# Attention and mixture of experts on one core: regrouping TensorE's work for a pair of heads by array split

## The chip, the core and the metric

The kernel runs on one core of a Trainium2 chip. The metric is the device time of one execution in microseconds (us). Three runs of the kernel before the change are known, and one further execution was taken by the hardware profiler. The core's engines are TensorE (PE, with weight loads shown as PEld), VectorE (DVE), ScalarE (ACT), GpSimd (POOL), and SyncE (SP), which issues most DMAs. All data are 32-bit floats.

## The reference

The input has 4 batches of 1024 tokens of width 256. A layer is causal attention with 16 heads, a residual and a layer norm, then 16 experts of which each token uses 3, a residual and a layer norm. Cut to the attention, which is all that the change touches:

```python
proj = x @ W_in.T + b_in                      # q, k, v: 16 heads of 64
q, k = rope(q), rope(k)                       # y_lo = lo*cos + hi*sin, y_hi = hi*cos - lo*sin
att = softmax(mask(q @ k.T / 8))              # 1024 x 1024, lower triangle
y = att @ v
x = layernorm(x + (y @ W_out.T + b_out))
x = layernorm(x + experts(x))                 # top 3 of 16, 256 -> 512 -> 256
```

## The kernel before

Heads are worked in pairs (`hh` is 0 or 1), 8 pairs a batch, 32 pairs `n` in all. After them come the experts. The loop over `n` stands in `attention`; the order of TensorE and VectorE inside it is written out by hand (`tc.manual_schedule` for PE and DVE), ScalarE, GpSimd and SP follow their dependencies and the program's order. Names that are used below:

- `project(n, i, g)` (L282 matmul `pp`, L287 on VectorE, L293 on ScalarE) makes q (`i` = 0) or k (`i` = 1) of pair `n` for 512 tokens `g`: two 128*128 matmuls, a product with `sin` and, on ScalarE, a plain copy `raw`. DMAs swap the copy's 32-row quarters into `swq` or `swk`. `rotate` (L321, L326, GpSimd) multiplies the swapped copy by `cos` and adds.
- `scores(n, qcs)` works the row blocks `qc` (128 queries each) of a chunk: 64*128 matmuls into PSUM banks `s` (L385), at most 512 columns each, for both heads; then on VectorE a reduction per bank (L393) that masks, copies to `p` and finds the row's extreme; then the exponential with row sums on ScalarE (L408). `divide` takes the reciprocal on VectorE (L422) and scales on GpSimd (L425).
- `turn` (L444) transposes 32x32 blocks of `p` on VectorE into `t_last` (keys 512 and up) and `t_first` (keys below 512).
- `product(n, j)` (L465) multiplies by v for key block `j` in 32*64 parts of the array, and adds up over `j` = 7 to 0 in four banks `y_ps`, of which 256 of 512 columns are used. `close` copies them out (`yT`, L479).
- `values` (L335 `vv`, L340) makes v for a pair two ahead, which goes through memory `v_d` and comes back as `vr` (`spread`). `out` (L489 `oo`) multiplies by W_out, a quarter of the tokens at a time, and VectorE adds the result to `acc` (L571).
- `fill` puts operations of the router and the layer norm of the batch before (`todo`) in between; `scatter` issues the router's indirect DMAs on GpSimd.

`pp`, `s`, `vv` and `oo` share four PSUM banks (`ps_s`), handed out in turn; `y_ps` has the other four. A pair's chunks are (7), (6), (5), (4), (3, 2), (1, 0), one per step `k` of the loop:

```python
for k in range(n_slots):
    ...
    if here:
        ends = scores(n, chunks[k])
    ...
    if k in (3, 4) and here:
        product(n, 10 - k)
    ...
    if k == 5 and here:
        product(n, 5)
    ...
    if k < 2 and before:
        product(n - 1, 4 - 2 * k)
        product(n - 1, 3 - 2 * k)
```

So products 7, 6 and 5 of pair `n` stand between its own later chunks, and 4 to 0 between the first chunks of pair `n + 1` (0 in step 2).

Of the kernel before, what the change touches and what calls it, by code (L numbers as in the profile page):

```python
# [119 lines left out]
def attention(  # L120
    tc, ap_, ident, eps_t, zero, router, sums, v_d,
# [4 lines left out]
    with ExitStack() as ctx:  # L126
# [7 lines left out]
        vp = pool("a_v", 3)  # L134
# [4 lines left out]
        pp = pool("a_p", 6)  # L139
        tp = pool("a_t", 1)  # L140
        yp = pool("a_y", 2)
# [11 lines left out]
        def load_x(b, g):  # L153
            xts[b, g] = xp.tile([P, DC, 512], FP, tag="xT", name="xT")
            return nc.sync.dma_start(out=xts[b, g], in_=xT_v[b, :, :, ts(g, 512)])
# [12 lines left out]
        def load_v(n):  # L168
            wv[n] = wp.tile([P, DC, 2 * P], FP, tag="wv", name="wv")
            return nc.sync.dma_start(out=wv[n], in_=w_v[n % NP // 2])  # L170
# [18 lines left out]
        mask = cp.tile([P, 512], FP, tag="mask")  # L189
        nc.gpsimd.memset(mask[:, : 512 - P], 0.0)  # L190
        make_causal_mask(nc, mask[:, 512 - P :], BIG / SCALE)
# [71 lines left out]
        raws, swps = {}, {}  # L263

        def project(n, i, g, kind=None):


            b, p = divmod(n, NP)
            if i == 0:
                half = rot[n, 0, g] = qkp.tile([P, 512], FP, tag=f"rotq{g}", name="rotq")  # L270
                part = raw = qkp.tile([P, 512], FP, tag="rawq", name="rawq")
                whole = True
            else:
                whole = n == 0 or (n, 1) in rot
                if (n, 1) not in rot:
                    rot[n, 1] = qkp.tile([P, T], FP, tag="rotk", name="rotk")
                    raws[n] = qkp.tile([P, T], FP, tag="rawk", name="rawk", bufs=1)
                half, raw = rot[n, 1][:, ts(g, 512)], raws[n]
                part = raw[:, ts(g, 512)]
# [14 lines left out]
            if whole:  # L294

                if i == 0:
                    swp = swps[n, 0, g] = qkp.tile([P, 512], FP, tag="swq", name="swq")
                else:
                    if (n, 1) not in swps:
                        swps[n, 1] = qkp.tile([P, T], FP, tag="swk", name="swk", bufs=1)  # L300
                    swp = swps[n, 1]
                if i and n == 0:
                    swp, raw = swp[:, ts(g, 512)], part
                for r in range(4):
                    (nc.scalar if i and n == 0 and g else nc.sync).dma_start(
                        out=swp[ts(r, 32), :], in_=raw[ts(r ^ 1, 32), :]
                    )
# [56 lines left out]
        def scores(n, qcs, kind=None):  # L364
# [3 lines left out]
            for hh in range(2):  # L368
                pr = pp.tile([P, T], FP, tag="p", name="p")
                at = 0  # L370
                for qc in qcs:
                    probs[n, qc, hh] = pr[:, ds(at, (qc + 1) * P)]
                    at += (qc + 1) * P
            for qc in qcs:
                w = (qc + 1) * P
                for k0 in reversed(range(0, w, 512)):
                    n_k = min(512, w - k0)
                    for hh in range(2):

                        if qcs == (1, 0) and qc == 0:  # L380
                            s = parts[hh][4][:, 2 * P :]
                        else:
                            s = ps_s.tile([P, 512], FP, tag="s", name="s")
                        parts.append((qc, hh, k0, n_k, s))
                        nc.tensor.matmul(  # L385
                            s[:, :n_k], lhsT=rot[n, 0, qc // 4][ts(hh, KD), ts(qc % 4, P)],
                            rhs=k[ts(hh, KD), ds(k0, n_k)], start=True, stop=True,
                        )
            nmax, ends = {}, []
            for qc, hh, k0, n_k, s in parts:  # L390
# [4 lines left out]
                    in1=mask[:, 512 - n_k :] if diag else zero[:, :n_k], scale=SCALE,  # L395
# [4 lines left out]
                if kind:  # L400
                    after(i, kind)
                order["scores"] = i
                if last:
                    pr = probs[n, qc, hh]
                    if hh == 0:
                        rsum = sp.tile([P, 2], FP, tag="rsum", name="rsum")
                        ends.append((qc, rsum))
                    order["exp"] = nc.scalar.activation(  # L408
                        pr, pr, AF.Exp, bias=m, scale=-1.0, accum_out=rsum[:, hh : hh + 1]
                    )  # L410
            return ends

# [73 lines left out]
        def out(n, h):  # L486
            ps = ps_s.tile([P, 2, D], FP, tag="s", name="oo")
            for v in range(2):
                nc.tensor.matmul(  # L489
                    ps[:, v, :], lhsT=st[n][:, ts(2 * h + v, P)], rhs=wo[n],  # L490
                    start=True, stop=True,
                )
            return accs[n // NP][:, ds(2 * h, 2), :D], ps
# [6 lines left out]
        chunks = [(7,), (6,), (5,), (4,), (3, 2), (1, 0)]  # L500
        n_slots = len(chunks)
        n_pairs = B * NP
        for i, g in ((0, 1), (1, 0), (1, 1), (0, 0)):
# [11 lines left out]
        with tc.manual_schedule(engines={mybir.EngineType.PE, mybir.EngineType.DVE}):  # L515
            for n in range(n_pairs + 2):
                b, p = divmod(n, NP)
                if n == 2:
                    load_router(Later(nc.vector, DVE, todo))
                for k in range(n_slots):  # L520
                    here, before, ahead = (one_of(n + i) for i in (0, -1, 1))
                    part, ends, last = None, [], "scores"
                    if before:
                        scatter(1 if k == 0 else 2 if k == 2 and here else 0)
                        if k == 0:
                            fill(ACT, 4.0)
                    if k == 2 and n <= n_pairs:
                        fill(DVE, 2.2, port=0.9)
                        fill(ACT, 4.0)
                    if k == 1:  # L530
                        fill(DVE, 0.7, True)
                    if here:
                        ends = scores(n, chunks[k])

                    m, kk = divmod(n * n_slots + k - 2, n_slots)
                    rows = [(qc, h) for h in (1, 0) for qc in chunks[kk] if qc >= 4 * h]

                    def turns(last):
                        qc, h = rows.pop(0)
                        for hh in range(2 if one_of(m) else 0):  # L540
                            turn(m, qc, hh, h, last)
                            last = "turn"
                        return last

                    if k == 2:
                        last = turns(last)

                    if k == 5:
                        fill(DVE, 0.6, True)
                    if k in (2, 5) and ahead:  # L550
                        project(n + 1, 0, int(k == 2), last)
                        last = "part"
                    if k == 2 and before:
                        product(n - 1, 0)
                        close(n - 1)
                    if k in (3, 4) and here:
                        product(n, 10 - k)
                    if k in (0, 3, 4, 5) and one_of(n - 1 - (k == 0)):
                        part = out(n - 1 - (k == 0), (k - 3) % 4 if k else 3)
                    if k in (3, 5):  # L560
                        fill(PE, 0.5 if k == 3 else 2.7)
                    if k == 5 and here:
# [776 lines left out]
```

## Time and profile before

| | |
|---|---|
| median of 3 runs | 1595.21 us (1595.2 to 1602.86) |
| profiled execution | 1580.36 us, its span 1578.5 us |
| granted TensorE clock in it | 0.982 |
| first pair's start to last pair's products | about 20 to 1126 us |
| experts, final norm and store | to 1578.5 us |

The views are read as follows. The page's first part gives busy time of each engine and its share of the span. The chain follows the work that ended last back from the end, so its shares name who set the time. A table by stage gives busy time in cut-out stretches. The timeline gives start and length of merged groups; the matmuls' ends are modelled, and one that starts before the last one's end overlaps it in the array's pipeline. An array split is written before the shape: 128*128, 64*128 or 32*64.

### The profile page before, as it was taken

What the parts mean: (1) busy time and instruction counts of PE and PEld (TensorE: products, weight loads), DVE (VectorE), ACT (ScalarE), POOL (GpSimd) and SP (SyncE); (2) the same over time, 40 slices, a digit from 0 to 9 for tenths busy, and PEclk for the clock granted to TensorE, in tenths of its full rate; (3) what the DMA queues carried; (4) which work ended last, traced back from release to release, by engine and by line L of the source; (5) the groups of instructions that cost most, each with busy time, mean ns of one, the idle gap of its engine ahead of it and who ended that gap; (6) DMA issues with size and microseconds to landing.
All of it is one profiled execution on the core that took longest, in us unless ns stands there. A gap on an engine that the chain in (4) does not pass through costs nothing.

```text
span 1578.5 us, 52463 instructions
## 1 busy us (share of the span) xinstructions
PE 1502.1 (95%) x20832; PEld 1047.0 (66%) x20832; DVE 1171.5 (74%) x3675; ACT 730.8 (46%) x1694; POOL 979.2 (62%) x928
## 2 busy tenths in 40 slices
PE   7999999999999999999999999999898999999970
PEld 4566666666666666666665666665687888888860
DVE  4888888898899999878999999889756333333324
ACT  3555555556555555655555557554431222222214
POOL 3775665775565677767766766678277843434435
PEclk9999999999999999999999999999999999999985
DMA  6464445546444554564465445545598998989866
GB/s 197 136 161 130 129 128 144 151 129 186 117 121 129 146 145 132 147 193 132 134 174 141 132 132 155 165 120 144 180 315 268 364 273 227 262 246 272 244 187 220
DMA packets 120041, 280.34 MB, mean 178 GB/s; under 512 B 21344, under 2 KB 64608, under 8 KB 108256
## 3 DMA queue, kind: packets, MB, share of 16 engines
q1 hardware_dynamic: 99872, 250.05, 52.9%
q0 software_dynamic: 19584, 26.62, 8.0%
q8 instruction: 166, 2.72, 0.8%
q14 instruction: 83, 0.68, 0.1%
q10 hardware_dynamic: 336, 0.27, 0.1%
HBM read 186.81 MB, written 61.09 MB: 157 GB/s over the span
## 4 chain that ended last, share of the span: by engine, by line
PE 86%; DVE 6%; issue 3%; DMA 3%; POOL 1%; ACT 1%; SPq 0%; ACTq 0%; POOLq 0%; DVEq 0%
PE y_ps L465 18%; PE s L385 17%; PE pp L282 14%; PE ps L1089 10%; PE ps L1073 10%; PE oo L489 7%; PE vv L335 7%; PE ps L1037 1%; DVE t_first L444 1%; DVE p L393 1%; PE lg_ps L706 1%; DMA sums<-y,ids 1%; DVE o_stats L1209 1%; POOL xs L803 1%; DMA vr<-v_d 1%
## 5 line engine op out<-in xcount | busy, mean ns | idle before, releaser
L425 POOL TENSOR_SCALAR p<-p,rinv 128x512 f32<-128x512 f32 (+7 forms) x512 | 374.6, 746 | 336.7 <-DVE rinv L422 291.9
L408 ACT ACTIVATE p<-p,nmax 128x512 f32<-128x512 f32 (+7 forms) x512 | 391.7, 766 | 411.9 <-DVE nmax L393 410.0
L385 PE MATMUL s<-rotk,rotq 64*128 64x512 f32 (+3 forms) x1536 | 309.6, 514 | 2.6 <-DVE rotk L318 2.0
L393 DVE CUSTOM_DVE_ANT_0 p<-s,mask 128x512 f32<-128x512 f32 (+3 forms) x512 | 224.2, 485 | 82.2 <-PE s L385 82.0
L444 DVE STREAM_TRANSPOSE t_first<-p 128x512 f32<-128x512 f32 (+3 forms) x512 | 276.1, 583 | 8.9 <-PE y_ps L465 8.8
L1104 POOL DMA_INDIRECT sums<-y,ids x104 | 163.5, 1572 | 181.1 <-DVE y L1100 121.3
L282 PE MATMUL pp<-xT,wqk 128*128 128x512 f32 x512 | 251.4, 614 | 9.2 <-DMA wqk<-in_w_qk_dram 5.5
L1078 ACT ACTIVATE hid<-ps,w 128x256 f32<-128x256 f32 (+1 forms) x224 | 89.7, 456 | 296.8 <-issue 244.3
L465 PE MATMUL y_ps<-t_first,vr 32*64 32x160 f32 (+2 forms) x8192 | 209.9, 338 | 4.3 <-DVE t_first L444 2.2
L465 PEld LDWEIGHTS y_ps<-t_first,vr 32*64 32x64 f32 x8192 | 165.9, 130 | 58.5 <-issue 44.2
L385 PEld LDWEIGHTS s<-rotk,rotq 64*128 64x128 f32 x1536 | 139.2, 186 | 97.7 <-issue 53.7
L1073 PE MATMUL ps<-xg,w 128*128 128x256 f32 (+1 forms) x896 | 191.7, 367 | 6.8 <-DVE xg L1040 6.8
L1094 DVE TENSOR_TENSOR y<-ps,w 128x512 f32<-128x512 f32 (+1 forms) x56 | 36.6, 653 | 212.9 <-PE ps L1089 175.4
L1089 PE MATMUL ps<-w,hid 128*128 128x256 f32 x832 | 188.8, 379 | 0.5 <-ACT hid L1078 0.5
L393 DVE CUSTOM_DVE_ANT_0 p<-s,zero,nmax 128x512 f32<-128x512 f32 x256 | 181.9, 748 | 2.9 <-PE s L385 0.7
L1073 PEld LDWEIGHTS ps<-xg,w 128*128 128x128 f32 x896 | 158.7, 192 | 25.5 <-DVE xg L1040 7.6
L282 PEld LDWEIGHTS pp<-xT,wqk 128*128 128x128 f32 x512 | 90.0, 190 | 126.1 <-issue 63.0
L1089 PEld LDWEIGHTS ps<-w,hid 128*128 128x128 f32 x832 | 157.2, 190 | 21.6 <-ACT hid L1078 0.7
L465 PEld LDWEIGHTS y_ps<-t_last,vr 32*64 32x64 f32 x7424 | 105.1, 130 | 76.5 <-issue 50.0
L489 PE MATMUL oo<-wo,yT 128*128 128x256 f32 x512 | 141.0, 398 | 2.6 <-ACT yT L479 1.4
L465 PE MATMUL y_ps<-t_last,vr 32*64 32x96 f32 (+3 forms) x7424 | 126.9, 248 | 0.5 <-DVE t_last L444 0.4
L803 POOL DMA_INDIRECT xs<-acc,slots x96 | 97.2, 1012 | 43.9 <-issue 21.8
(187 smaller groups left out, 1726.9 us busy)
## 6 DMA issues: line engine op xcount, KB each, us to landing
w<-in_wall_dram SPq DMA_DIRECT2D x56, 1154.0 KB
vr<-v_d SPq DMA_DIRECT2D x256, 128.0 KB
vr<-v_d SPq DMA_DIRECT2D x128, 256.0 KB
swq<-rawq SPq DMA_DIRECT2D x256, 64.0 KB
v_d<-v SPq DMA_DIRECT2D x128, 128.0 KB
swk<-rawk SPq DMA_DIRECT2D x124, 128.0 KB
x<-xs SPq DMA_DIRECT2D x48, 264.0 KB
wqk<-in_w_qk_dram SPq DMA_DIRECT2D x32, 256.0 KB
```

What stands on the lines that cost most here:

```text
L282: nc.tensor.matmul(ps, lhsT=wqk[n][:, c, i, :], rhs=xts[b, g][:, c, :], start=(c == 0), stop=(c == DC - 1),)
L385: nc.tensor.matmul(s[:, :n_k], lhsT=rot[n, 0, qc // 4][ts(hh, KD), ts(qc % 4, P)], rhs=k[ts(hh, KD), ds(k0, n_k)], start=True, stop=True,)
L393: i = nc.vector.tensor_tensor_reduce(out=probs[n, qc, hh][:, ds(k0, n_k)], in0=s[:, :n_k], in1=mask[:, 512 - n_k :] if diag else zero[:, : ...
L408: order["exp"] = nc.scalar.activation(pr, pr, AF.Exp, bias=m, scale=-1.0, accum_out=rsum[:, hh : hh + 1])
L425: order["divide"] = router.behind = nc.gpsimd.tensor_scalar(pr, pr, rinv[:, hh : hh + 1], 1.0, ALU.mult, ALU.mult)
L444: order["turn"] = router.on_dve = after(nc.vector.transpose(turned[n][h][:, hh, :, ds(i - 4 * h, n_j, step=7 - 4 * h), :], probs[n, i, hh] ...
L465: nc.tensor.matmul(st[n][a][ts(hh, KD), ds(32 * j, 32 * (TC - j))], lhsT=v[ts(a, 32), c * 8 + 2 * u + jh % 2, ts(hh, KD)], rhs=t[ts(a, 32) ...
L489: nc.tensor.matmul(ps[:, v, :], lhsT=st[n][:, ts(2 * h + v, P)], rhs=wo[n], start=True, stop=True,)
L803: i = nc.gpsimd.indirect_dma_start(out=self.xs, out_offset=bass.IndirectOffsetOnAxis(ap=st["slots"][:, r, c : c + 1], axis=0), in_=acc[:, ...
L1073: nc.tensor.matmul(ps[:, f - f0, :], lhsT=w[:, ds(c * FF + f * P, P)], rhs=xg[:, c, :n], start=(c == 0), stop=(c == DC - 1),)
L1089: nc.tensor.matmul(ps[:, h, :], lhsT=hid[:, f, ts(h, P)], rhs=w[:, ds(W2_AT + f * D, D)], start=(f == 0), stop=(f == FC - 1),)
L1104: s = behind(nc.gpsimd.indirect_dma_start(out=sums_of(t), out_offset=bass.IndirectOffsetOnAxis(ap=ids[:, h : h + 1], axis=0), in_=y[:, h, ...
```

## The change

The six steps of a pair become four groups. The five chunks 4, 3, 1, 0 and 2 are multiplied in one run, with product 7 ahead of it; the 128*128 work of that part follows in one run, then products 6, 5 and 4; products 3 to 0 stand in the next pair, after chunk 6. `multiply` (the matmuls) is split from `scores` (reductions and exponentials), and `bank` puts the scores of row blocks 1 and 0 and the 128 diagonal columns of block 4 into unused columns of the `y_ps` banks. Exponentials can be held back (`hold`, `release`) so that they are issued later on ScalarE. `out` takes two pairs at once and adds both up in PSUM, so that VectorE adds to `acc` once for two pairs; `plan` says where. The divisions of chunk (1, 0) are issued in the next pair. Each swapped half of k goes out by itself. To fit memory, buffers change: the probabilities have one buffer for each chunk and head, `wv`, one half of `xT`, one half of the rotated q and the swapped q are single, `yT` has three, mask and zeros share a tile, and three tiles of the router share one (`wide`).

```diff
-        pp = pool("a_p", 6)
+        pp = pool("a_p", 1)
...
-        yp = pool("a_y", 2)
+        yp = pool("a_y", 3)
...
+            part = qkp.tile([P, 512], FP, tag="raw", name="raw")
...
+                swp = swps[n, 0, g] = qkp.tile([P, 512], FP, tag="swq", name="swq", bufs=1)
...
+            for r in range(4):
+                (nc.scalar if i and n == 0 and g else nc.sync).dma_start(
+                    out=swp[ts(r, 32), :], in_=part[ts(r ^ 1, 32), :]
+                )
...
+        def bank(n, qc, hh, k0):
+            y = st.get(n)
+            if qc == 4 and k0:
+                return y[2 + hh][:, 3 * P :], False
+            if qc == 1:
+                return y[hh][:, 2 * P :], False
+            if qc == 0:
+                return y[2 + hh][:, 2 * P : 3 * P], False
+            return ps_s.tile([P, 512], FP, tag="s", name="s"), True
...
-        def out(n, h):
+        def out(pairs, h):
             ps = ps_s.tile([P, 2, D], FP, tag="s", name="oo")
             for v in range(2):
...
+                for n in pairs:
+                    nc.tensor.matmul(
+                        ps[:, v, :], lhsT=st[n][:, ts(2 * h + v, P)], rhs=wo[n],
+                        start=(n == pairs[0]), stop=(n == pairs[-1]),
+                    )
...
+                if here:
+                    ends = scores(n, (7,), multiply(n, (7,)), hold)
+                    release(1)
+                if before:
+                    divide(n - 1, ends10, last)
+                if ahead and n > 0:
+                    project(n + 1, 1, 0, last)
...
+                last = turns(n - 1, [(3, 0)], last)
+                for o in outs.get((n, 0), []):
+                    parts.append(out(*o))
...
+                if here:
+                    ends = scores(n, (6,), multiply(n, (6,)))
+                last = turns(n - 1, [(2, 0), (1, 0), (0, 0)], last)
...
+                if ahead:
+                    project(n + 1, 1, 1, last)
...
+                for j in reversed(range(4 if before else 0)):
+                    product(n - 1, j)
+                if before:
+                    close(n - 1)
...
+                last = turns(n, [(7, 1)], last)
+                if n <= n_pairs:
+                    fill(DVE, 2.4, port=0.6)
...
+                if here:
+                    ends5 = scores(n, (5,), multiply(n, (5,)), hold)
+                    release(1)
+                last = turns(n, [(7, 0)], last)
+                if ahead:
+                    project(n + 1, 0, 1, last)
+                release()
+                if here:
+                    product(n, 7)
...
+                if here:
+                    ends4 = scores(n, (4,), multiply(n, (4,)))
+                    p3 = multiply(n, (3,))
+                    small = multiply(n, (1, 0))
+                    ends32 = scores(n, (3, 2), p3 + multiply(n, (2,)), hold)
+                    divide(n, ends5, "scores")
+                    ends10 = scores(n, (1, 0), small, hold)
+                    release(2)
+                if vals:
+                    values(m, vals[0])
+                release(2)
+                last = turns(n, [(6, 1)], last)
+                if here:
+                    divide(n, ends4, last)
+                if ahead:
+                    rotate(n + 1, 0, 1)
+                last = turns(n, [(5, 1)], last)
+                if ahead:
+                    project(n + 1, 0, 0, last)
...
+                product_out()
...
+                last = turns(n, [(4, 1)], last)
+                if here:
+                    divide(n, ends32, last)
...
+                last = turns(n, [(6, 0)], last)
+                if vals:
+                    values(m, vals[1])
...
+                last = turns(n, [(5, 0), (4, 0)], last)
+                if ahead:
+                    rotate(n + 1, 0, 0)
...
+                if here:
+                    for j in (6, 5, 4):
+                        product(n, j)
+                if p < 2:
+                    fill(DVE, 2.0 - 0.6 * p)
```

## The prediction

> **What bounds the kernel now.** I read the page first: engine shares and the chain.
>
> ```profile
> PE 1502.1 (95%) x20832; PEld 1047.0 (66%) x20832; DVE 1171.5 (74%) x3675; ACT 730.8 (46%) x1694; POOL 979.2 (62%) x928
> PE 86%; DVE 6%; issue 3%; DMA 3%; POOL 1%; ACT 1%; SPq 0%; ACTq 0%; POOLq 0%; DVEq 0%
> ```
>
> TensorE carries 86% of the chain. The whole-span share mixes attention and experts, so next comes the table by stage, cut at the first product of four neighbouring pairs.
>
> ```profile
> core 0: us, PE busy (x) PEld busy (x) DVE busy (x) ACT busy (x) POOL busy (x), PEclk, DMA share, GB/s
> 105.20:139.00 33.80, 33.80 (x588) 21.18 (x586) 29.19 (x89) 18.24 (x44) 21.36 (x22) 1.00 0.44 121
> sum 135.00, PE 135.00 PEld 84.64 DVE 116.60 ACT 72.78 POOL 85.45; mean PE 33.75 PEld 21.16 DVE 29.15 ACT 18.19 POOL 21.36
> ```
>
> A pair takes 33.75 us and TensorE is busy for all of it; VectorE has 4.6 us to spare, GpSimd 12.4. TensorE's waits between 100 and 1060 us say the same:
>
> ```profile
> PE pp L282 <- DVE nmax L393: 2.2, 4, 1.4
> PE y_ps L465 <- issue: 0.2, 1, 0.2
> ```
>
> So a pair is as long as TensorE's instruction stream, and anything off TensorE is worth nothing until it makes TensorE wait. What can the stream lose without losing matmuls? The timeline of TensorE (start, length, line):
>
> ```profile
> 283.59 1.98 PE L282 MATMUL pp<-xT,wqk 128*128 128x512 f32 x4
> 285.41 1.03 PE L489 MATMUL oo<-wo,yT 128*128 128x256 f32 x4
> 286.37 1.05 PE L465 MATMUL y_ps<-t_last,vr 32*64 32x96 f32 x64
> ...
> 292.09 1.19 PE L465 MATMUL y_ps<-t_last,vr 32*64 32x128 f32 x63
> 293.02 0.29 PE L465 MATMUL y_ps<-t_first,vr 32*64 32x160 f32 x1
> ...
> 293.04 1.35 PE L465 MATMUL y_ps<-t_first,vr 32*64 32x160 f32 x63
> 294.32 1.77 PE L385 MATMUL s<-rotk,rotq 64*128 64x384 f32 x8
> 296.03 1.98 PE L282 MATMUL pp<-xT,wqk 128*128 128x512 f32 x4
> 297.94 3.07 PE L465 MATMUL y_ps<-t_first,vr 32*64 32x192 f32 x128
> 300.94 1.56 PE L385 MATMUL s<-rotk,rotq 64*128 64x256 f32 x8
> ```
>
> Add start and length and compare with the next start. pp ends at 285.57 and oo, of the same split (128*128), starts at 285.41, 0.16 before. oo ends at 286.44 and the product, of another split (32*64), starts at 286.37, only 0.07 before. A change of split costs 0.09 us there. Inside products it costs more: product 4 ends at 293.28 and product 3 starts at 293.02, 0.26 before; product 3 ends at 294.39 and the scores start at 294.32, 0.07 before: 0.19 us.
>
> **The gain.** I write S7 for the score chunk of row block 7, Y7 for product 7, pp/vv/oo for the 128*128 work. Before, a pair's ring is S5, pp, Y0, S4, Y7, oo vv, S3 S2, Y6, oo vv, S1 S0, pp oo, Y5, S7, oo pp, Y4 Y3, S6, pp, Y2 Y1: 18 changes. After: S5, pp, Y7, S4 S3 S1 S0 S2, vv pp oo vv, Y6 Y5 Y4, S7, pp oo, S6, pp, Y3 to Y0: 11 (the change's words say 12). In the built programs' order on TensorE I count 572 changes before and 352 after, 220 fewer, 7 for each of 31 pairs. Of the 7, four are ends of scores or 128*128 work (4 x 0.09 = 0.36) and three ends of product runs (3 x 0.09 to 0.19 = 0.27 to 0.57). Together 0.63 to 0.93, taken at 0.80 (the product seams are nearer to the measured 0.19), so 31 x 0.80 = 25 us, between 20 and 29. Matmuls are as many as before: two pairs added up in PSUM still need all of theirs.
>
> **What could take it back: the burst.** Four score banks feed all scores and 128*128 work. Five chunks in a run, with no product between them, must find their banks emptied by VectorE. The change gives them help: S1, S0 and the diagonal 128 columns of S4 go to free columns of the product banks. I walk one pair from the start of S5 (t = 0). TensorE, start to start from the timeline and the chain of waits: S5 1.49, pp 1.91, Y7 0.66, S4 1.39, S3 plus S2 1.70, S1 plus S0 0.85, vv, pp and oo 1.73 to 1.82 each. VectorE, from its own timeline at the same place before:
>
> ```profile
> 301.67 0.42 DVE L393 CUSTOM_DVE_ANT_0 p<-s,mask 128x256 f32<-128x256 f32 x1 [2.21 <-PE s L385]
> ...
> 303.88 1.30 DVE L444 STREAM_TRANSPOSE t_last<-p 128x512 f32<-128x512 f32 x2
> 305.10 0.71 DVE L287 SCALAR_TENSOR_TENSOR rotq<-pp,bqk,sin 128x512 f32<-128x512 f32 x1
> ```
>
> VectorE begins S5 0.73 after TensorE (300.94 to 301.67, after idling 2.21), leaves it at 2.94 and needs 1.22 for a transpose pair. Hence:
>
> ```
> t (us)      TensorE                 VectorE
> 0 - 4.06    S5, pp, Y7              S5 0.73-2.94, transposes -4.16, rotq -4.87
> 4.06- 8.00  S4 S3 S1 S0 S2          S4 4.87-6.8, S3 -8.0
> 8.00-15.1   vv pp oo vv             S2 8.2-9.1, S1 S0 -10.3, transposes 6,5 (last half) -11.9, rotq -12.6, 4 -13.2
> 15.1-17.7   Y6 Y5 Y4                sum -14.2, six 128x512 transposes (0.65 each) -18.1
> 17.7-       S7                      S7 from 18.75 (1.05 after its start)
> ```
>
> Where TensorE needs a bank: the second half of S3 takes pp's, free when ScalarE's copy of it ends (4.87 + 0.05 + 0.69 = 5.6), and TensorE is there at 5.45 + 0.43 = 5.9. S2 takes S4's two, free at 6.1 and 6.8, needed at 7.26. The first vv takes S3's, free at 7.4, needed at 8.0. Y4 needs the transpose that ends at 13.2, at about 16.8. S7's reductions find VectorE free 0.65 early. In the second half of the pair the tightest is S6's last bank, freed by the output sum 0.3 ahead. So: no wait, but margins of 0.3, 0.5, 0.6 and 0.3 us on a TensorE that has had none to lose.
>
> **Other parts.** Output sums: 128 become 68, 60 x 0.659 = 40 us off VectorE; off the path, worth 0, but without them the last margin (0.65) is gone. The reciprocal of S5's sums now stands behind the reductions of S4, S3 and S2 on VectorE, so GpSimd starts that division at 9.2. Behind it stand 640's division and the rotation of the next q: 9.2 + 2 x 0.90 + 2 x 0.80 + 2 x 1.275 = 15.2 against S7 at 17.7. The other q rotation, after the divisions and up to three scatters of 1.01, ends by 23.5 and is needed at S3 of the next pair, near 38. The divisions of S1 and S0 wait for the next S7 and end by 25.5, for transposes near 28. Swapped k goes out in eight DMAs of 64 KB, not four of 128; at some 0.6 us an issue in the trace, 2.4 us more on SP, which issues some 30 a pair. The swap buffer for q is single now, so four DMAs on SP wait for GpSimd's rotation (15.2); behind them are v stores, the next pair's swapped k and v loads, of which the first to be needed, v for Y7, has over 10 us. All of these at 0; if a cover fails each costs what its margin lacks, 0 to 1 us a pair. Fill work of 2.0 and 1.4 us is put right before S7 in two pairs of three batches, where the margin is 0.65: 0 to 1.2 us each, 0 to 7 us, taken at 3. First pair and last: the first product rows come later, past the wait for v that holds TensorE 2 us at 55 us; the last pair has less 128*128 work over the same VectorE chain (TensorE was already idle some 6 us there): 0, between -4 and +4. The experts after it start earlier by the same amount.
>
> **A rule against it.** The Trainium skill, TensorEngine Tiling (Array Packing), PSUM Bottleneck, says that tiling makes TensorE faster but not the evacuation of PSUM, which may then be the bottleneck. Taken at its word the run is paced by its reductions (1.8 + 2.2 + 1.1 us in the table's rows against 3.94 of TensorE, 1.1 a pair), and the sum would be 31 x (1.1 - 0.8) = +9, 1604 us. The walk gives 0 for it, because 7 us of vv, pp and oo follow at once, in which VectorE catches up.
>
> **Sum.** The profiled execution took 1580.4 (span 1578.5); 1580.4 - 25 + 3 = 1558. The median of the three runs, 1595.2, is 14.8 above it, and the trace does not show why; I carry the difference over: 1595.2 - 22 = 1573. Its own range: -29 - 4 to -20 + 7 + 4, so 1562 to 1586.
>
> **Rivals.**
> 1. The margins are partly eaten: one of the 0.3 us margins misses by 0.5 to 0.8 us in each pair, and the saving goes into a wait for VectorE. Then 1588 to 1603. For: four margins below 0.7. Against: VectorE's rows repeat to a few hundredths from pair to pair. Chance 0.12.
> 2. Slower: the run starves for banks. Place: S3's second half to the first vv. In the first pair, where no products lie between the chunks, 8 matmuls of S7 run 329 ns apart, not 200: about 0.8 us more for a chunk. If S4, S3 and S2 pay that, 2.3 us a pair, the result is 31 x (2.3 - 0.8) = +47, 1642; at two of them +25, 1620. It decides once VectorE comes to S4 more than 0.8 us later than the 4.87 of the walk. Against: there VectorE had S7 and S6 in a row with 512-wide parts alone. Chance 0.13.
> 3. The change does less than it says: the seams cost 0.09 throughout and joined products overlap no better. Then 220 x 0.09 = 20 us, 1575 to 1586, still inside the forecast; no chance of its own.
> 4. More: VectorE's 40 us also remove the waits around the router's fill work, where pairs took up to 36.5 us: another 8 us, 1560 and below. Chance 0.04.
>
> **Numbers.** Forecast 0.71, rivals 0.12, 0.13 and 0.04. A measurement here tells about 0.5% (8 us) from no change. Faster by more: 0.71 + 0.04 = 0.75; within: 0.12; slower: 0.13. The range of 8 in 10 takes the forecast's range, a few us below it, and rival 1: 1556 to 1602.
>
> **What would show it.** In the new profile: pairs at 32.8 to 33.1 us; TensorE busy for all of them; products 6, 5, 4 and 3 to 0 each in one piece, each starting 0.13 to 0.26 before the last has ended; VectorE about 28 us a pair. Wrong: a TensorE row waiting on the row reductions or on ScalarE's copy of pp in every pair (rivals 1, 2), or pairs at 33.1 with no such waits (rival 3).

## The result, and the profile after

The changed kernel is slower: a median of 1665.97 us in 4 runs (1664.46 to 1672.13), the kernel before 1596.33 us beside it. The ratio is 1.0435, with a 95% interval of 1.0395 to 1.0475. The prediction was 1573 us, 1556 to 1602. The profiled execution took 1664.49 us; its span is 1662.7 us.

The page's engine shares and its chain, as first read of the kernel before:

```profile
PE 1528.9 (92%) x20832; PEld 1086.7 (65%) x20832; DVE 1144.2 (69%) x3615; ACT 719.7 (43%) x1694; POOL 981.6 (59%) x927
PE 84%; issue 5%; DVE 5%; DMA 2%; ACT 2%; POOL 1%; another core or an unknown queue 0%; ACTq 0%; SPq 0%; POOLq 0%; DVEq 0%
```

The instructions on TensorE are as many as before (20832), yet its busy time grew from 1502.1 to 1528.9 and its share fell. The other part that grew is `issue`, time in which the engine waited for nothing that the profile shows: 5% of the chain. VectorE is busy 27 us less, and nobody gained by it. The table by stage for three pairs in a row, cut at the start of Y7 (columns as in the prediction's table):

```profile
149.90:183.20 33.30, 33.30 (x589) 22.15 (x588) 28.34 (x88) 17.97 (x44) 20.42 (x22) 1.00 0.48 119
183.20:218.70 35.50, 33.73 (x585) 22.24 (x584) 27.94 (x86) 17.55 (x43) 22.47 (x23) 1.00 0.53 144
218.70:253.90 35.20, 33.75 (x589) 22.07 (x588) 28.17 (x87) 17.78 (x44) 22.53 (x23) 1.00 0.50 129
```

The first of them runs without a gap and beats the 33.75 of before; the next two have TensorE idle for 1.77 and 1.45 us. VectorE takes 28 us, as predicted. TensorE's waits between 100 and 1060 us (total, times, longest) say where:

```profile
PE y_ps L476 <- issue: 36.9, 46, 2.3
PE s L377 <- ACT raw L293: 6.5, 4, 1.9
PE pp L282 <- DVE nmax L396: 2.5, 2, 2.0
```

The wait that the prediction feared, `pp` for VectorE's reductions, stayed at 2.5 us (2.2 before). The new one sits inside the products and had been 0.2. The timeline of TensorE shows one of these gaps, in products 3 to 0:

```profile
242.74 5.27 PE L476 MATMUL y_ps<-t_first,vr 32*64 32x160 f32 x230
249.47 1.07 PE L476 MATMUL y_ps<-t_first,vr 32*64 32x256 f32 x18 [1.45 <-issue]
250.47 0.49 PE L377 MATMUL s<-rotk,rotq 64*128 64x256 f32 x2
```

No buffer changes hands at 248.0: the run stops 18 matmuls before its end and goes on 1.45 us later. In the trace of the DMA queues a 16 KB packet of queue 8, kind `instruction`, ran from 246.65 to 247.90, and the run resumed 1.57 us after its end. This queue has 166 packets in both kernels. If it is TensorE's, as the ends of the gaps say, its 41664 instructions of PE and PEld are 251 to a packet, some 125 matmuls with their weight loads.

```profile
q8 instruction: 166, 2.72, 0.7%
```

Of the 28 gaps over 0.6 us in the products between the first and the last Y7 (35.1 us in all), 24 end 1.2 to 1.6 us after such a packet; packets start 6.7 us apart there in the median, so this is no chance. In the trace of before there is one gap over 0.6 us in products (0.8 us), and it waits for v.

I went on with the attention part alone: from the first to the last start of Y7 (31 pairs) it took 1062.5 us before and takes 1142.8 now, 80 us more; what lies before and behind it grew by 4 us together. These 84 us are more than the 70 between the medians, because the profiled execution before took 1580.4 us, some 16 less than the median of its kernel here.

### The profile page after: what moved, and what is told of

Same layout as the page of the kernel before. It is cut to its first block, busy times and chain, and to the rows that moved or that the text cites. A ratio compares the mean times of both kernels' runs of the same rounds, so it can differ in the third digit from the quotient of the medians.

```text
span 1662.7 us, 52506 instructions
## 1 busy us (share of the span) xinstructions
PE 1528.9 (92%) x20832; PEld 1086.7 (65%) x20832; DVE 1144.2 (69%) x3615; ACT 719.7 (43%) x1694; POOL 981.6 (59%) x927
## 4 chain that ended last, share of the span: by engine, by line
PE 84%; issue 5%; DVE 5%; DMA 2%; ACT 2%; POOL 1%; another core or an unknown queue 0%; ACTq 0%; SPq 0%; POOLq 0%; DVEq 0%
PE y_ps L476 19%; PE s L377 15%; PE pp L282 14%; PE ps L1161 10%; PE ps L1177 10%; PE vv L325 7%; PE oo L501 6%; PE y_ps L377 2%; PE ps L1125 1%; DVE p L396 1%; DVE t_first L455 1%; PE lg_ps L792 1%; DMA sums<-y,ids 1%; DVE o_stats L1297 1%; ACT p L411 0%
## 5 line engine op out<-in xcount | busy, mean ns | idle before, releaser
L377 PE MATMUL s<-rotk,rotq 64*128 64x512 f32 (+2 forms) x1152 | 312.0, 581 | 12.5 <-ACT raw L293 7.1
L396 DVE CUSTOM_DVE_ANT_0 p<-s,mask 128x512 f32<-128x512 f32 (+2 forms) x320 | 171.3, 580 | 185.2 <-PE s L377 185.2
L282 PE MATMUL pp<-xT,wqk 128*128 128x512 f32 x512 | 257.1, 626 | 11.1 <-DMA wqk<-in_w_qk_dram 5.7
L455 DVE STREAM_TRANSPOSE t_first<-p 128x512 f32<-128x512 f32 (+3 forms) x512 | 266.4, 578 | 0.0
L476 PE MATMUL y_ps<-t_first,vr 32*64 32x160 f32 (+3 forms) x8192 | 208.0, 338 | 20.2 <-issue 18.1
L476 PEld LDWEIGHTS y_ps<-t_first,vr 32*64 32x64 f32 x8192 | 175.0, 131 | 61.3 <-issue 52.8
L1161 PE MATMUL ps<-xg,w 128*128 128x256 f32 (+1 forms) x896 | 193.9, 369 | 6.1 <-DVE y L1188 4.0
L377 PEld LDWEIGHTS s<-rotk,rotq 64*128 64x128 f32 x1152 | 125.9, 190 | 102.5 <-issue 54.4
L396 DVE CUSTOM_DVE_ANT_0 p<-s,mask,nmax 128x512 f32<-128x512 f32 x256 | 181.9, 747 | 10.7 <-PE s L377 8.1
L311 POOL TENSOR_TENSOR swk<-swk,cos 128x1024 f32<-128x1024 f32 x31 | 73.4, 2367 | 135.8 <-DMA swk<-raw 116.1
L325 PE MATMUL vv<-wv,xT 128*128 128x256 f32 x512 | 126.8, 392 | 5.0 <-DMA wv<-in_w_v_dram 5.0
```

Of the source, the lines that this page charges most:

```text
L282: nc.tensor.matmul(ps, lhsT=wqk[n][:, c, i, :], rhs=xts[b, g][:, c, :], start=(c == 0), stop=(c == DC - 1),)
L325: nc.tensor.matmul(ps[:, u, :], lhsT=xts[b, cc // 2][:, c, ts(cc % 2 * 2 + u, P)], rhs=wv[n][:, c, :], start=(c == 0), stop=(c == DC - 1),)
L377: nc.tensor.matmul(s[:, :n_k], lhsT=rot[n, 0, qc // 4][ts(hh, KD), ts(qc % 4, P)], rhs=k[ts(hh, KD), ds(k0, n_k)], start=own, stop=True, s ...
L396: i = nc.vector.tensor_tensor_reduce(out=probs[n, qc, hh][:, ds(k0, n_k)], in0=s[:, :n_k], in1=mask[:, 512 + P - n_k :] if diag else zero[ ...
L455: order["turn"] = router.on_dve = after(nc.vector.transpose(turned[n][h][:, hh, :, ds(i - 4 * h, n_j, step=7 - 4 * h), :], probs[n, i, hh] ...
L476: nc.tensor.matmul(st[n][a][ts(hh, KD), ds(32 * j, 32 * (TC - j))], lhsT=v[ts(a, 32), c * 8 + 2 * u + jh % 2, ts(hh, KD)], rhs=t[ts(a, 32) ...
```

## The experiments

Three theories were put up. **Fetch**: a long run of small matmuls uses instructions faster than queue 8 brings them. **Scatter**: beside GpSimd's scatters TensorE gets through small matmuls slowly. **Rows**: the prediction's rival, score chunks that wait for VectorE or ScalarE. All ratios are to the kernel before on the same chip (1581.6 to 1598.8 us), so times of different experiments are compared by their ratios where the chips differ; differences to the changed kernel, given in us, are uncertain by some 5 us.

**1. Product runs cut in two.** Y4 goes behind S7 of the next pair, Y1 and Y0 behind its S5.

```diff
+                    product(n - 1, 4)
...
-                for j in reversed(range(4 if before else 0)):
+                for j in reversed(range(2 if here else 0, 4) if before else ()):
...
+                    for j in reversed(range(2 if before else 0)):
+                        product(n - 1, j)
...
-                    for j in (6, 5, 4):
+                    for j in (6, 5):
```

> The changed kernel with both product runs cut in two: Y4 is moved behind the next pair's S7, and Y1 Y0 behind S5, so that no run holds more than two products in a row. Fetch theory (TensorE runs out of instructions inside the long runs of products, about 30 gaps of 0.3 to 2.3 us each after a transfer on the instruction queue): the gaps go, about 40 us of idle and part of the half-clock windows behind them (5 to 10), less four more split changes in a pair at 0.09 to 0.19 us (30 x 0.56 = 17): 25 to 55 us under the changed kernel, 1610 to 1640. Row theory (the chunks of scores starve for banks because VectorE and ScalarE are late): the gaps are not in the products, so nothing goes but 17 us come: 1675 to 1690. Scatter theory (the products are slow only where a scatter runs beside them): the gaps stay where a scatter runs, within 15 us of the changed kernel.

1657.5 us, ratio 1.0355 [1.0315, 1.0396]: only 8 us gained. By its time alone this is what the scatter theory said (within 15 us); the fetch theory's range was missed. The edit adds two split changes to a pair (11 to 13), not four. By pairs the reading is plain. The table by stage, a pair early in the attention part and one late:

```profile
178.40:211.60 33.20, 33.20 (x589) 21.76 (x588) 28.30 (x86) 17.86 (x42) 21.76 (x23) 1.00 0.54 144
717.40:757.30 39.90, 37.77 (x589) 24.06 (x588) 29.94 (x93) 18.88 (x45) 24.61 (x26) 0.96 0.48 128
```

Pairs 3 to 6 run at 33.18 each, without a gap (the cut points of the table are rounded). The late pairs got worse, since the edit had moved Y4 to where three scatters are issued. Y4 takes 1.13 to 1.18 us in every pair without scatters but the first, and 2.94 to 5.76 in ten of the twelve with three; in the other two (1.14 and 1.27) no scatter ran beside Y4. A Y4 without scatters, then one with them:

```profile
193.43 1.21 PE L476 MATMUL y_ps<-t_last,vr 32*64 32x128 f32 x64
...
646.77 0.97 PE L476 MATMUL y_ps<-t_last,vr 32*64 32x128 f32 x47
647.42 1.07 POOL L899 DMA_INDIRECT xs<-acc,slots  x1 [0.16 <-issue]
647.91 0.45 PE L476 MATMUL y_ps<-t_last,vr 32*64 32x128 f32 x3 [0.17 <-issue]
648.64 0.46 PE L476 MATMUL y_ps<-t_last,vr 32*64 32x128 f32 x4 [0.28 <-issue]
648.80 0.97 POOL L899 DMA_INDIRECT xs<-acc,slots  x1 [0.30 <-issue]
649.40 0.41 PE L476 MATMUL y_ps<-t_last,vr 32*64 32x128 f32 x3 [0.30 <-issue]
650.08 0.97 POOL L899 DMA_INDIRECT xs<-acc,slots  x1 [0.30 <-issue]
650.10 0.50 PE L476 MATMUL y_ps<-t_last,vr 32*64 32x128 f32 x2 [0.29 <-issue]
650.86 1.10 PE L476 MATMUL y_ps<-t_last,vr 32*64 32x128 f32 x5 [0.26 <-issue]
```

64 matmuls in one piece without scatters. With them, 47 in the first group; from the first scatter on, two to five in each 0.7 us. The clock is not what slows them: the granted clock falls to half only at 650.0 us, behind the first slow groups, and the Y4 at 811 us took 4.77 us at the full clock.

**2. All four scatters together, behind the rotation of k and so beside S4 to S2.**

```diff
+                    router.behind = order["rotated"]
+                    scatter(4)
```

> The changed kernel with all four scatters of a pair issued together on GpSimd, after the rotation, so that they run beside the scores S4 to S2 and not beside products. Scatter theory (beside GpSimd's scatters TensorE gets through 27 to 51 products in 3.6 us in place of about 200): 20 to 35 us under the changed kernel, 1630 to 1645. Fetch theory alone (gaps only from the length of the runs): the gaps stay, within 8 us of the changed kernel. Row theory: GpSimd's divisions come later by 4 us, turns and products behind them too: 5 to 30 us above.

1656.8 us, ratio 1.0372 [1.033, 1.0414], 9 us less: between what the two theories said. The long runs kept their gaps (`issue` 31.8 us, before the edit 36.9), and four scatters in a run hold GpSimd for 4.9 us. In the trace of experiment 4 they land more often beside the 128*128 run that follows S4 to S2 than beside those scores. What that holds up shows where the runs are cut as well (experiment 4): S7 waits for rotated q.

**3. ScalarE's copy ahead of S7's second exponential.**

```diff
+                    after(order["exp"], "raw")
```

> The changed kernel with one order changed on ScalarE: the copy of pp (k, second half of the columns) comes before the second exponential of S7, not behind both. If S6's last bank waits for that copy (0.33 us in each pair by the trace): S6's time in the trace goes from a median of 2.03 back to about 1.70, and the kernel is 8 to 15 us under the changed one. If S6 waits for the output sum, as the prediction had it, or for S7's row reductions: no change, or up to 10 us slower because S7's row is normalized 0.9 later.

1663.1 us, ratio 1.0409 [1.0375, 1.0444]: no change clear of noise, and S6 stayed at 2.03 us. My reading was wrong. The timeline of this run around S6:

```profile
239.08 0.69 ACT L293 ACTIVATE raw<-pp,bqk 128x512 f32<-128x512 f32 x1 [0.22 <-DVE rotk L287]
239.91 2.10 PE L377 MATMUL s<-rotk,rotq 64*128 64x384 f32 x8
240.18 0.65 DVE L509 TENSOR_TENSOR acc<-oo,acc 128x512 f32<-128x512 f32 x1
```

The copy is over before S6 starts; the output sum ends at 240.83, 0.92 after S6's start, and S6's last bank is begun at 0.98. So the prediction had named the right wait; only its margin was not 0.3 ahead but 0.3 behind (2.03 against 1.70).

**4. The three edits together.**

> The three edits together (products in runs of two, scatters together behind the rotation, the copy ahead of S7's second exponential). If the three causes are separate and make up the loss: the sum of the three differences, 60 to 100 us under the changed kernel, 1565 to 1605, so about the time of the kernel before. If they are one cause (the gaps come only where a long run and a scatter meet): no more than the larger of the first two, 1610 to 1640.

1628.7 us, ratio 1.0164 [1.0131, 1.0197]: 37 us less. That is four times the larger of the first two, so not one cause, and short of the 60 that three separate ones were expected to give. It is more than the three alone (8, 9 and 3), by more than noise perhaps; in the traces' attention part it is 32 against 6, 13 and 3. I read it so that the first two need each other: a cut run gains only if its pieces do not land beside scatters (Y4 takes 1.13 to 1.94 us here in all pairs). `issue` in the products went to 1.1 us; the longest wait is now for GpSimd, which has the scatters ahead of its rotation:

```profile
PE s L377 <- POOL rotq L316: 15.2, 7, 2.7
PE y_ps L476 <- issue: 1.1, 3, 0.5
```

**5. Each cause put alone into the kernel before.** The long run:

```diff
-                        spread(n, 1, 0)
...
-                    if k < 2 and before:
-                        product(n - 1, 4 - 2 * k)
-                        product(n - 1, 3 - 2 * k)
+                    if k == 1 and before:
+                        for j in (4, 3, 2, 1):
+                            product(n - 1, j)
+                    if k == 1 and one_of(n):
+                        spread(n, 1, 0)
```

> The kernel before with one edit: its products Y4 Y3 and Y2 Y1 of a pair, which stand in two runs of 2.2 and 3.0 us, are put into one run of 5.2 us at the place of the second. Nothing else of the change. Switch theory (the prediction's: fewer split changes, and the stream of TensorE is the sum of its matmuls): one product run less, 0.28 us in a pair, 9 us faster, 1588. Fetch theory (a long run of products uses up its instructions faster than the instruction queue brings them): a gap on `issue` in most pairs' joined run, 0.6 to 1.2 us each, and none of that kind elsewhere: 10 to 30 us slower, 1607 to 1627.

The scatters:

```diff
-                        scatter(1 if k == 0 else 2 if k == 2 and here else 0)
+                        scatter((4 if here else 1) if k == 0 else 0)
...
-                    if k == 5 and here:
+                    if k == 5 and here and not before:
                         scatter(1)
```

> The kernel before with one edit: the four scatters of a pair, which it spreads over three places beside scores and projections, are issued in a run at the first place, where products Y4 Y3 (2.23 us) are what TensorE does next. Nothing else of the change. In the run with the split product runs, a product of 1.14 us took 2.94 to 5.76 in the pairs where three scatters ran beside it. Scatter theory: in the 12 or so pairs with scatters Y4 Y3 take 4.5 to 7 us, 25 to 60 us slower in all, 1622 to 1657. Fetch theory alone (length of run only): Y4 Y3 stay at 2.23 and what is lost is what the later divisions cost, 0 to 15 us.

The joined run: 1669.5 us, ratio 1.0438 [1.041, 1.0465], worse than any theory said. TensorE's waits:

```profile
PE s L385 <- DVE acc L571: 20.7, 26, 0.8
PE y_ps L465 <- issue: 14.1, 27, 1.7
PE pp L282 <- DVE nmax L393: 9.0, 27, 1.3
```

The gaps came as the fetch theory says: Y4 to Y1 took 193.9 us in 30 pairs, and had taken 160.8 as two runs; all 11 gaps over 0.6 us on `issue` in them end 1.2 to 1.6 us after an instruction packet, with the granted clock full throughout. Half of the loss is another: with Y4 Y3 gone from between S7 and S6, S6 waits for the output sum and goes from 1.70 to 3.08 us. The product run had been the cover of a bank.

The scatters: 1628.4 us, ratio 1.0185 [1.0162, 1.0208], as the scatter theory said. Y4 Y3 take 2.23 us in every pair without scatters but the first, and 3.3 to 8.3 in the eleven with them. The first of these:

```profile
636.37 0.99 POOL L803 DMA_INDIRECT xs<-acc,slots  x1 [0.30 <-issue]
636.47 0.95 PE L465 MATMUL y_ps<-t_last,vr 32*64 32x128 f32 x44
637.66 0.97 POOL L803 DMA_INDIRECT xs<-acc,slots  x1 [0.31 <-issue]
637.67 0.45 PE L465 MATMUL y_ps<-t_last,vr 32*64 32x128 f32 x4 [0.24 <-issue]
638.42 0.44 PE L465 MATMUL y_ps<-t_last,vr 32*64 32x128 f32 x4 [0.31 <-issue]
```

**6. Other places, with long and with cut runs.** Three scatters (two beside S4 to S2, one ahead of S7), `oo` and its sum ahead of `pp`, the first pair's vv later (the last is not shown; the order on ScalarE of experiment 3 is in both kernels too):

```diff
+                    router.behind = order["rotated"]
+                    scatter(2)
...
-                if ahead and n > 0:
-                    project(n + 1, 1, 0, last)
...
                     parts.append(out(*o))
...
+                if ahead and n > 0:
+                    project(n + 1, 1, 0, last)
```

> The changed kernel with three edits and its long product runs left as they are: three of a pair's scatters only, two beside the scores S4 to S2 and one beside S7; the output sum's oo ahead of pp, so that VectorE's sum no longer frees S6's last bank late; in the first pair vv later, so that it does not wait 5 us for its weights. If run length is a cause of its own: the gaps on `issue` stay at 25 to 35 us, 1620 to 1640. If the gaps come from scatters and waits around them: 1575 to 1600.

> The same three edits and the product runs cut in two as in the first experiment. By the sum of the causes: steady pairs at 33.18 less 0.3 for S6, about 32.9 against 33.75 of the kernel before (20 to 25 us over 30 pairs), and the pairs with scatters and layer norm as before the change or up to 1 us worse each: 1570 to 1595, faster than the kernel before by 0.2 to 1.6%. If the causes were named wrongly: no lower than 1625.

1689.3 us (ratio 1.0565 [1.0544, 1.0587]) with long runs, 1664.6 (1.0417 [1.0388, 1.0447]) with cut ones. Cutting the runs is worth 25 us here. Both are slower than expected. My order of `oo` and `pp` was bad: S6 went from 2.03 to 3.42 us in both, and `pp` waits for VectorE 26 times, as the waits of the run with cut ones show:

```profile
PE pp L282 <- DVE nmax L396: 17.4, 26, 0.7
PE oo L501 <- ACT raw L293: 11.2, 1, 11.2
PE y_ps L476 <- issue: 3.6, 13, 0.4
```

**7. The same places without that order, and no scatters at all.** The second edit is that of the last two kernels; the one that fills the rows at the start, and those that the first shares with experiments 1, 3 and 4, are not shown.

```diff
+                        scatter(2)
...
-                scatters.pop(0)()
+                scatters.pop(0)
```

> Product runs cut in two, the copy ahead of S7's second exponential, as in the run of all three edits; but the output sum's place left as in the changed kernel, three scatters in a pair, two beside S4 to S2 and one ahead of S7, and pair 0 without the two vv of pair 2 (pair 1 does all four). From the run of all three edits (1628.7): the 12 pairs with scatters lose about 1.2 us each, as in the last run, not 4.5 (40 us less), and pair 0 some 5 us less: 1575 to 1600. If the loss beside scatters is not what made those pairs long: 1620 to 1635.

> The changed kernel without the scatters of the first three batches (left out: those rows are filled with the padding row at the start, so the experts compute on padding). Its long product runs are as they are. Scatter theory alone: no gaps on `issue` are left, the pairs from 17 on run like the pairs before. Both causes: the gaps that follow an instruction packet by about 1.46 us stay, 20 to 30 us of them, in early and late pairs alike, and the attention part (first to last Y7) goes from 1143 us to 1105 to 1125.

> The same without scatters, with the product runs cut in two. Both causes: no gaps on `issue` at all, Y4 at 1.14 us in every pair, pairs at 33.2 but for those with layer norm and routing: the attention part 1070 to 1085 us against 1137 with scatters (1062.5 in the kernel before). If the long pairs after 17 come from routing on VectorE and ScalarE and not from the scatters: 1110 or more.

The first: 1618.6 us, ratio 1.0238 [1.0216, 1.026] (1581.7 before on that chip). That is above its range, and by the ratio slower than experiment 4, although pairs 19 to 23, all with scatters, now take 33.6 to 34.1 us. Pair 0's edit took 0.7 us off it and made pair 1 longer by 3.6, and one pair takes 48.5 us. In the waits around that pair GpSimd stands before the residual, whose buffer is still being loaded:

```profile
ACT raw L293 <- DVE rotq L287: 12.4, 1, 12.4
POOL acc L208 <- DMA acc<-in_x_dram: 8.1, 1, 8.1
```

The two without scatters took 1858.2 and 1830.7 us, since filling the rows at the start holds v back by some 214 us in pair 1; the pairs after it can be read. With long runs the gaps are still there, without them they are gone; TensorE's waits from 400 to 1330 us in the two:

```profile
PE y_ps L476 <- issue: 29.5, 30, 1.8
```

```profile
PE y_ps L476 <- issue: 0.6, 2, 0.3
```

All 22 gaps over 0.6 us of the first (26.8 us) end 1.2 to 1.6 us after an instruction packet, and no scatter stands beside them. So long runs lose time without scatters, and in experiment 5 scatters do in a run that loses nothing without them. Whether a scatter, too, works through the supply of instructions is not shown.

**8. What was still open.** Fewer scatters spread so that they end before their source buffer is loaded again, and, in the kernel before, one product run less where no run gets long: Y6 is put right ahead of Y5.

```diff
+                    scatter(2 + n % 2)
```

```diff
-                    if k in (3, 4) and here:
+                    if k == 3 and here:
...
+                        product(n, 6)
```

> Like the last combined run, but pair 0 as in the changed kernel and three or four scatters in a pair (two or three behind the rotation, one ahead of S7), so that all rows of a batch are written before the buffer that they are read from is loaded again. If the 48.5 us pair of that run (9.4 us for ScalarE's copy) came from scatters that ran on into the reload: that pair falls to 36 to 38 and the first pairs by 5, 1595 to 1610 against 1597 of the kernel before, so no slower than it by over 0.8%. If it came from the order on ScalarE: the long pair stays, 1610 to 1625.

> The kernel before with one product run less and no long one: Y6 (0.9 us) is moved behind S0's neighbours to Y5, so that Y6 Y5 stand in one run of 1.9 us. Two split changes less in a pair, 0.28 us by the trace. Fetch theory: a run of 1.9 us makes no gaps, so if nothing loses its cover 6 to 9 us faster, 0.4 to 0.6%. If Y6 was the cover of the row reductions around it (as Y4 Y3 was of a chunk of 1.7 us that went to 2.9): that chunk waits 0.3 to 1.2 us, 0 to 30 us slower.

The first: 1603.5 us, ratio 1.0138 [1.0123, 1.0154]; the long pair fell to 39.0, with the order on ScalarE as it was, so the reload had been its cause. The time lies in its range, but the kernel before takes 1581.6 us on this chip, not 1597, so the 0.8% that it was allowed were missed. By the ratio it is the best form of the change that I found (experiment 4's interval overlaps with it), and still slower than the kernel before. The second: 1583.05 us, ratio 1.0011 [1.0002, 1.002], no gain. It saves one split change in a pair (18 to 17), not two. Its products did get shorter (Y6 Y5 1.66 us, apart 0.90 + 0.98 = 1.88), but from the start of S3 S2 to the start of the `oo` that now follows at once it takes 1.93, not 1.70: Y6 had stood between them, and `oo` now waits for a bank that VectorE has not left.

```profile
PE oo L489 <- DVE nmax L393: 3.9, 20, 0.3
```

## Why the prediction was wrong

The account of the 80 us of the traces, by the 31 pairs (start of Y7 to start of the next):

| pairs | before | after | runs cut | no scatters | no scatters, runs cut |
|---|---|---|---|---|---|
| 0 | 32.6 | 40.9 | 39.6 | 40.6 | 38.5 |
| 1 to 7 | 236.1 | 244.4 | 231.4 | | |
| 8 to 10 | 106.3 | 116.9 | 114.1 | 113.7 | 114.6 |
| 11 to 15 | 170.7 | 174.7 | 166.7 | 174.3 | 166.6 |
| 16 to 30 | 516.9 | 566.1 | 585.1 | 541.9 | 532.1 |

Scatters: 566.1 - 541.9 = 24 us. These two traces are of different chips (1596 and 1582 us for the kernel before), so up to some 15 of the 24 can be the chip's: in pairs 0 to 15 the chip does not show (545.6 us in the scatter run of experiment 5, on a chip of 1598.7, and 545.7 before), in those behind it may. Long runs: 1.3 + 13.0 + 2.8 + 8.0 in pairs 0 to 15 (after less runs cut), 9.8 in 16 to 30 (the last two columns), 35 us. The other numbers compare executions of one level in pairs 16 to 30. The rest, 80 - 24 - 35 = 21, is the form without gaps and scatters against the kernel before: 17 us gained in pairs with nothing else in them, if all 30 had their 0.57, and so some 38 lost in pair 0 and in the pairs with layer norm and routing.

- *"What bounds the kernel"*: right on the kernel before, wrong in what I drew from it. "A pair is as long as TensorE's instruction stream" took the stream to be its matmuls' time. The stream also has to be brought: gaps on `issue` of some 30 us stand in the products, and the long runs cost 35 us in all, at 0 in the sum. This is the step that failed first: "Matmuls are as many as before" says nothing on how closely they stand.
- *"The gain"*: the mechanism holds, and the size about: the sum's 0.80 for 7 changes is 0.11 a change. The one pair without gaps that is shown (33.30) gives as much: 0.45 gained and 0.33 lost in S6, over 7. With cut runs a pair has 13 split changes, 5 less than before, and takes 33.18, not 33.75, although S6 loses 0.33: (0.57 + 0.33) / 5 = 0.18 us a change, if nothing else differs; 0.22 for the one product run less in the last experiment. But it is a gain only where nobody waits at the end of it; there `oo` waited for as much.
- *"The burst"*: the walk was nearly right. S5 takes its 1.49 us, and S4 to S2 take 3.98 in the median and 3.71 with cut runs, against 3.94 in the walk. The one margin of its four that failed is the last, "S6's last bank, freed by the output sum 0.3 ahead": 0.3 behind, 0.33 us in each pair, some 10 us. Rival 1 described such a wait, at 0.5 to 0.8 us a pair. Rival 2 got the sign, not the mechanism; its mark, `pp` or vv waiting for reductions in every pair, is not in the trace. Its price, 329 ns a matmul, was read from 21.2 to 23.5 us, where the granted clock was 0.5 from 22.0 us on. Two more figures of the rivals do not come out of their terms: 31 x 0.8 gives 1598 for rival 1, not 1603, and 8 us gives 1565 for rival 4, not 1560.
- *"Other parts"*: the second failure. "Up to three scatters of 1.01" were costed by GpSimd's time and its order alone, at 0. What they do to the engine beside them was not asked, though the change puts Y0 and the joined products beside them, where `pp` and score chunks had been. They cost 24 us in the account above, or some 10 if the chip's level is taken off; in experiment 5, on one chip, putting them beside Y4 and Y3 cost 30.
- *"First pair and last: 0, between -4 and +4"*: 8 us in pair 0 alone, 1.3 of them the long run's. `wv` is a single buffer after the change: its second load is issued at 46.2 us, when the first vv are done (at 5.3 us in the kernel before, where nothing waits for it), and vv waits 5.0 us for it. The page's row of vv:

```profile
L325 PE MATMUL vv<-wv,xT 128*128 128x256 f32 x512 | 126.8, 392 | 5.0 <-DMA wv<-in_w_v_dram 5.0
```

  Taking that wait away gains little by itself: in experiment 7's first run, with these vv in pair 1, a score chunk of pair 0 waits 7.1 us for GpSimd's rotated q.
- *"Fill work ... taken at 3"*: 10.6 us in pairs 8 to 10, 2.8 of them the long runs'. Of the other 7.8, which the runs-cut trace shows, 4.2 are waits of TensorE that the kernel before does not have there: 1.8 for ScalarE's copy of `pp`, 1.7 for its copy `yT`, 0.7 for rotated q. What makes the rest, and whether layer norm on ScalarE or the router is behind it, was not separated.
- *The rule weighed*: the Trainium skill, TensorEngine Tiling (Array Packing), PSUM Bottleneck, taken at its word, would have had the run paced by its reductions, 1.1 us a pair. The trace does not show it: the scores S4 to S2 that were to pace it take 3.98 us, not 5.1. The sum by that rule, 1604 us, is nearer to the result, but for another cause.
- A rule that I had not weighed: the Trainium skill, Runtime: NRT & Kernel Launch, Instruction fetch mechanics, says that instructions come in 16 KiB blocks of 256 and that the cost of crossing a block is mostly hidden. The trace agrees on the block (16384 bytes, 251 instructions) and not on "mostly hidden": 22 gaps over 0.6 us in the run with long runs and no scatters, 26.8 us from 400 to 1330 us.

That the gaps are fetch rests on three things: they end a fixed time after an instruction packet, they come back when a run of the kernel before is made long, and they go when runs are cut. Why the packet comes late was not tried; that a long run outruns the packets is the reading that fits the rows below. Why a scatter slows small matmuls is open too.

## What to carry to other kernels

An engine's stream has a supply as well as a length: before small instructions are put side by side, count them against the instruction queue's packets in the trace, and keep the runs short enough that slower instructions follow. Work of another engine that was harmless beside large matmuls has to be costed again when small ones are moved beside it. And a saving on the bounding engine is worth only what the next wait leaves of it: each product between two score chunks was also the time in which a bank was emptied.

## What the runs showed of the hardware

- Of 166 instruction packets, no two start less than 3.09 us apart in any of the fifteen traces, while 251 instructions of products 6 to 4 can be used up in 1.7 us (a matmul with its load every 11 to 15 ns) and of products 3 to 0 in 2.1 to 3.4 (every 17 to 27 ns). That 3.09 us is a floor was not tried. Runs of 2.6 us (Y3 Y2) and 3.4 us (Y1 Y0) showed hardly any of these gaps; in the changed kernel Y6 to Y4 took 2.6 to 2.8 us in 15 pairs and 4.0 to 8.0 in the other 17, and Y3 to Y0 (5.8 at best) took 7.0 in the median.
- Beside GpSimd's indirect DMAs TensorE did 12 matmuls of 32*64 in the 2.95 us from 647.91 in the timeline above. In the run of experiment 4 it did 18 to 27 of 128*128 or 64*128 in 4.9 us in ten of twelve such stretches and was never idle, and 28 of 128*128 took 7.09 us beside four scatters (from 747 us) as without any (from 859 us): no cost was seen beside large matmuls.
- Windows of half the clock, 3.4 to 6.8 us each, stand in the changed kernel seven times between 40 and 1180 us, and never there in the kernel before. Four of the seven begin in or right behind an idle time of TensorE of 1.9 to 5 us, but behind four others of 1.9 to 2.3 us (610, 832, 986 and 1064 us) there is none, so a gap of this length does not decide it. What the windows cost was not measured.
